# A scan kernel of two layers: the phases of layer 0 in another order, one more joint pair of row scans in layer 1, the last column quarter summed by halves

## The chip, the core and the metric

One core of a Trainium2 chip runs the whole program. The metric is the device time of one execution in microseconds (us), lower is better; it is given as the median of several runs. TensorE (PE in the profile, its weight loads PEld) does the matrix products, VectorE (DVE), ScalarE (ACT) and GpSimd (POOL) work element by element, and transfers are issued from the queues of SyncE (SP), ACT and POOL.

## The reference

Two layers of the same kind, on x of 32 images, 48 channels, 64 rows, 128 columns, in float32:

```
x = x + scans(groupnorm(x))          # 16 groups of 3 channels, per image; twice, with other weights
step:  next = inp + conv1d(carry, w, 5 taps, 48x48 channels, padding 2) + b
scans: D: down over the 64 rows;  U: up again over D's rows, same weights
       R: right over the 128 columns of U;  L: left over R
```

Each step needs the step before it, so a layer is a chain of 63 + 63 steps over rows and 127 + 127 over columns. Images are independent of each other, and U must be complete over the rows before R can begin for the same images.

## The kernel before, in words

**Work.** The images are four groups of eight. A row scan takes one group: a row of it is three tiles of 128 partitions (48 channels times 8 places along the convolved direction, 384 in all) by 128 elements. A column scan takes a pair of groups, and a column of it is of the same size. A step (`step`, L941 to L970) is nine products, each in two matmul instructions, and three additions on VectorE (L968), which add bias and input and write the next row or column in place. The next step's products read it.

**Phases.** `PHASES` lists twelve phases: four row phases (down and up for one group) and two column phases (right and left for a pair) in each layer. Layer 0 goes rows 0, rows 1, columns of pair 0, rows 2, rows 3, columns of pair 1. Layer 1 does all rows first. The step tiles are named after it: step_02d is layer 0, group 2, down; step_01r is layer 0, pair 1, right. A phase in `JOINED` shares its down scan with the up scan of the phase before: one joint step does both, with 256 elements in each product, by the same weights (`two_row_step`). Before, phases 8 and 9 are joined: group 2 down with group 1 up, and group 3 down with group 2 up, in layer 1.

**Memory.** The scanned data lie in three slots of SBUF. A row phase holds rows 0 to 31 of its group in one slot and rows 32 to 63 in another; the three slots change roles from phase to phase. A column phase takes the 128 columns in four quarters of 32; each quarter has six units (three tiles, times the two groups of the pair, its halves). What leaves the slots goes to DRAM and comes back in another layout: the normalized input (xin), the rows after U (upa in layer 0, upb in layer 1), the result of layer 0 (mid).

**The seam.** Where a column phase follows the second row phase of its own pair (`follows`), its first quarter cannot be read from DRAM in time. The first rows are then sent from slot to slot directly (`send_row`, `send_rest`: transfers arena<-arena) when the up scan ends. This is so for both column phases of layer 0 before, and for none in layer 1.

**The order of all other work.** `at(t, fn)` writes a task into an agenda; t counts steps, a joint step as two. Before each step the tasks that are due are issued, and every engine and queue keeps that order (`in_order`). An engine waits at a task for its data, with all that stands behind it. The tasks that matter here:
- `plan_input` (L1089): brings one group of x in. Six blocks of four rows per partition: `take_in` (one transfer arena<-in_x, into the one buffer), `permute` on GpSimd (L712), `put_out` (xin<-arena), and `take_others` on ScalarE (L583 sums, L575 squared deviations). Then `scaling`, a chain of small operations spread over about ten steps; it begins with a sum over ScalarE's results on VectorE (L600) and, where its slack is 0, goes on there with L605, which needs the squares as well.
- `plan_rows` (L1109): loads the rows of a group in four parts of 16 rows (`move_rows`: 20 transfers arena<-xin each), scales them on ScalarE (`scale_rows`, L797: 24 instructions for 16 rows), and writes the rows after U (`move_rows`: ten transfers upa<-arena per 8 rows). I call one such transfer a piece.
- `plan_cols` (L1169): loads and spills quarters; for each unit, the residual is loaded and added on GpSimd (L889), the result kept in mid, and its statistics taken for the next layer's normalization: half 0 on VectorE (L628), half 1 on ScalarE (`ResultStatsA`: L651, L654, L657, eight plus one plus eight instructions for a unit).

## Time and profile before

| | |
|---|---|
| runs | median 4161.74 us of 3, from 4159.11 to 4164.88 |
| profiled execution | 4154.44 us, of it 4152.7 between first and last instruction |
| mean granted clock of TensorE | 0.987 |
| VectorE, ScalarE, GpSimd busy | 2075.8 us (50%), 1307.4 (31%), 832.1 (20%) |
| transfers | 680.86 MB, of 2213904 packets 2014096 under 512 B |

The profiled execution is 7.3 us below the median of the runs. A step of a scan is seen in the profile as 18 matmuls on L954 and three VectorE operations on L968. The time of a scan without waits is its number of steps times the time of a step; anything above that is a wait, and the idle time noted in brackets in the timeline, with what ended it, says of whom. A row of a timeline has the start, the length, the engine, the line, the operation, what it writes and reads, the count, and in brackets the idle time before it. A row of the table by stretches has the borders, the length, then busy time and number of instructions for PE, PEld, DVE, ACT, POOL, the granted clock, the share of the DMA engines and GB/s.

### The profile page before, as it was taken

The numbers are of one execution on the slowest core, as the hardware profiler recorded it, in microseconds if no ns is written. First come the engines' busy times: TensorE is split into PE (matmuls) and PEld (weight loads), VectorE is DVE, ScalarE is ACT, GpSimd is POOL, SyncE is SP. The second block draws the span as 40 slices with busy tenths as digits, with TensorE's granted clock in tenths as the row PEclk, the third lists the DMA queues.
The fourth block names the chain that finished last, engine by engine and source line by source line (L and its number), as shares of the span: only waits on it lengthen the run. The fifth ranks groups of instructions, "written<-read, shape, count | busy, mean of one in ns | idle before, by whom it ended". The sixth has DMA issues, their size and how long they took to land. (4 is left out here: it accounts for less than half of the span.)

```text
span 4152.7 us, 85830 instructions
## 1 busy us (share of the span) xinstructions
PE 4021.1 (97%) x34360; PEld 3934.6 (95%) x34360; DVE 2075.8 (50%) x6124; ACT 1307.4 (31%) x2630; POOL 832.1 (20%) x745
## 2 busy tenths in 40 slices
PE   6999989899999999999999999999999999999994
PEld 5999989899999999999999998888999999999994
DVE  6454444457655444445656443333444444444444
ACT  4646001436884500003584534443000002200122
POOL 5631010333421001002412000000000015610354
PEclk9999999999999999999999999999999999999997
DMA  9897779769978966913997975666599029999799
GB/s 298 223 188 147 121 129 211 225 150 277 198 189 179 146 115 117 216 41 93 255 172 145 141 114 95 99 104 105 95 167 216 1 59 256 302 241 154 147 234 194
DMA packets 2213904, 680.86 MB, mean 164 GB/s; under 512 B 2014096, under 2 KB 2162816, under 8 KB 2188928
## 3 DMA queue, kind: packets, MB, share of 16 engines
q1 hardware_dynamic: 2069376, 582.40, 68.4%
q10 hardware_dynamic: 141568, 87.46, 8.7%
q0 software_dynamic: 2560, 5.51, 0.5%
q8 instruction: 271, 4.44, 0.5%
q14 instruction: 129, 1.06, 0.1%
HBM read 398.32 MB, written 295.14 MB: 167 GB/s over the span
## 5 line engine op out<-in xcount | busy, mean ns | idle before, releaser
L889 POOL TENSOR_TENSOR arena<-arena 128x2048 f32<-128x2048 f32 x80 | 362.8, 4549 | 1519.5 <-PE step_10l L954 474.3
L797 ACT ACTIVATE arena<-arena,offsetr,scaler 128x128 f32<-128x128 f32 (+1 forms) x576 | 345.0, 688 | 352.5 <-DMA arena<-mid 244.6
L797 ACT ACTIVATE arena<-arena,offset,scale 128x256 f32<-128x256 f32 (+2 forms) x360 | 249.3, 788 | 155.7 <-DMA arena<-xin 131.7
L712 POOL COPY arena<-arena 128x256 f32<-128x256 f32 x340 | 200.9, 652 | 470.7 <-DMA arena<-in_x 451.5
L954 PE MATMUL step_00r<-arena,early 128*128 128x128 f32 x2286 | 254.3, 275 | 25.2 <-DVE arena L968 14.3
L954 PEld LDWEIGHTS step_00r<-arena,early 128*128 128x128 f32 x2286 | 253.1, 186 | 26.1 <-DVE arena L968 15.0
L651 ACT ACTIVATE early<-arena 128x256 f32<-128x256 f32 x192 | 129.5, 675 | 453.2 <-POOL arena L889 446.9
L954 PE MATMUL step_01r<-arena,early 128*128 128x128 f32 x2286 | 251.4, 273 | 6.9 <-DMA arena<-arena 5.4
L954 PEld LDWEIGHTS step_01r<-arena,early 128*128 128x128 f32 x2286 | 250.7, 185 | 7.6 <-issue 5.7
L954 PE MATMUL step_11r<-arena,early 128*128 128x128 f32 x2286 | 249.2, 272 | 0.0
L954 PEld LDWEIGHTS step_11r<-arena,early 128*128 128x128 f32 x2286 | 248.7, 184 | 0.5 <-DVE arena L968 0.3
L954 PE MATMUL step_10r<-arena,early 128*128 128x128 f32 x2286 | 248.7, 272 | 0.1
L954 PEld LDWEIGHTS step_10r<-arena,early 128*128 128x128 f32 x2286 | 248.5, 184 | 0.2 <-DVE arena L968 0.2
L954 PE MATMUL step_10l<-arena,wleft 128*128 128x128 f32 x2286 | 248.5, 272 | 0.0
L954 PE MATMUL step_11l<-arena,wleft 128*128 128x128 f32 x2286 | 248.5, 272 | 0.0
L954 PE MATMUL step_00l<-arena,wleft 128*128 128x128 f32 x2286 | 248.4, 272 | 0.0
L954 PE MATMUL step_01l<-arena,wleft 128*128 128x128 f32 x2286 | 248.4, 272 | 0.0
L954 PEld LDWEIGHTS step_10l<-arena,wleft 128*128 128x128 f32 x2286 | 248.4, 184 | 0.0
L954 PEld LDWEIGHTS step_11l<-arena,wleft 128*128 128x128 f32 x2286 | 248.4, 184 | 0.0
L954 PEld LDWEIGHTS step_00l<-arena,wleft 128*128 128x128 f32 x2286 | 248.4, 184 | 0.0
L954 PEld LDWEIGHTS step_01l<-arena,wleft 128*128 128x128 f32 x2286 | 248.4, 184 | 0.0
L911 ACT COPY arena<-arena 128x256 f32<-128x256 f32 x172 | 99.7, 656 | 360.5 <-POOL arena L889 249.5
(565 smaller groups left out, 6912.9 us busy)
## 6 DMA issues: line engine op xcount, KB each, us to landing
xin<-arena SPq DMA_DIRECT2D x94, 512.0 KB, 5.5
arena<-in_x SPq DMA_DIRECT2D x18, 2048.0 KB, 9.6
arena<-xin SPq DMA_DIRECT2D x96, 384.0 KB, 10.8
upb<-arena SPq DMA_DIRECT2D x192, 192.0 KB, 3.9
arena<-upb SPq DMA_DIRECT2D x96, 384.0 KB, 11.0
arena<-xin SPq DMA_DIRECT2D x174, 192.0 KB, 4.3
mid<-arena SPq DMA_DIRECT2D x32, 1024.0 KB, 11.7
upa<-arena SPq DMA_DIRECT2D x168, 192.0 KB, 3.9
```

What stands on the lines that cost most here:

```text
L651: nc.scalar.activation(junk[:, 0:n], view[:, b], AF.Identity, accum_out=self.sum[:, i, j : j + 1])
L712: copy(dst[:, r, q], src[:, r0 + r, q])
L797: nc.scalar.activation(args[0], args[0], AF.Identity, bias=args[2], scale=args[1])
L889: eng.tensor_tensor(unit, unit, nat, ALU.add)
L911: copy(by_w(perm)[:, a], src[:, a])
L954: nc.tensor.matmul(part(turn(whole(ps[o]))[0:m], -s), weights[:, i, at : at + m], part(turn(src(i)), s), start=seen[o] == 1, stop=seen[o] ...
```

## The change

Four things change. In layer 0 all four row phases come first, then both column phases, as in layer 1; so neither column phase follows the rows of its own pair, and the seam is used nowhere. In layer 1 phase 7 is joined too: group 1 down runs with group 0 up. The last quarter of the second column phase is added and measured by halves: the three units of half 1 right after the scan, those of half 0 later, since the joined phase 7 puts its first rows into the places of half 1. And the tasks get other times: groups 2 and 3 of the input are brought in during the row phases 01 and 02, six blocks 11.5 steps apart (13 before), each load 5.5 steps ahead of its permutation (7 before); the slack of the scaling of group 2 goes from 4 to 0; the weights of the columns and of layer 1 are loaded in later phases; where a row phase of layer 0 follows another, the first two parts of its rows are loaded three and four steps earlier and scaled two and three steps earlier.

```diff
 PHASES = (
     ("rows", 0, 0),
     ("rows", 0, 1),
-    ("cols", 0, 0),
     ("rows", 0, 2),
     ("rows", 0, 3),
+    ("cols", 0, 0),
     ("cols", 0, 1),
...
-JOINED = (8, 9)
+JOINED = (7, 8, 9)
...
             if g > 1:
-                at(t - 7, take_in, g, rows * j, nat)
+                at(t - 5.5, take_in, g, rows * j, nat)
...
-        spread(t, scaling(f"x{g}", 0, g, stats, (0, 0, 4, 0)[g]), 1)
+        spread(t, scaling(f"x{g}", 0, g, stats, 0), 1)
...
             if not PHASES[k][1]:
-                ahead, scaled = (-33, -22, 0, 11), (-16, -5, 16, 30)
+                ahead, scaled = (-36, -26, 0, 11), (-18, -8, 16, 30)
...
-            first, every = left + 34 + 32 * n_done, 4.5
-            if j == 0 and PHASES[k + 1 if not final else k][0] == "rows":
-                first, every = (end + 29, 6) if pair else (first, 7)
-            units += [(first + every * i, j, i) for i in range(n)]
+            first = left + 34 + 32 * n_done
+            times = [(first + 4.5 * i, i) for i in range(n)]
+            if j == 0 and not final and PHASES[k + 1][0] == "rows":
+                times = [(end + 3 + 7 * i, 2 * i + 1) for i in range(NG)]
+                times += [(end + 28 + 6 * i, 2 * i) for i in range(NG)]
+            units += [(t, j, i) for t, i in times]
...
-            spread(units[-1][0] + (14 if pair else 70), pair_scaling(pair, stats, 8), 1)
+            spread(units[-1][0] + 14, pair_scaling(pair, stats, 8), 1)
...
-    times = [starts[1] + 36] + [starts[2] + 45 + 13 * j for j in range(5)]
+    times = [starts[1] + 24 + 11.5 * j for j in range(6)]
     plan_input(2, times, 6, 6, nats, tiles[2:4])
-    times = [starts[2] + 116 + 13 * j for j in range(2)]
-    times += [starts[3] + 42 + 13 * j for j in range(4)]
+    times = [starts[2] + 24 + 11.5 * j for j in range(6)]
     plan_input(3, times, 6, 6, nats, tiles[2:4])
...
-    at(starts[1] + 50, more_weights, "right", 0, RIGHT)
-    at(starts[1] + 54, more_weights, "left", 0, LEFT)
-    at(starts[3] + 50, more_weights, "down1", 1, DOWN)
+    at(starts[3] + 50, more_weights, "right", 0, RIGHT)
+    at(starts[3] + 54, more_weights, "left", 0, LEFT)
+    at(starts[5] + 70, more_weights, "down1", 1, DOWN)
```

Two places show what this does to the order. The first is ScalarE where layer 1 begins (10d). L797 is the scaling of group 0's rows; L651, L654 and L657 together are the statistics of one unit of half 1 (sum_r, neg_r, dev_r). Before:

```order
L797 ACTIVATE arena<-arena,offsetr_12864,scaler_12863 128x256 x24
L651 ACTIVATE early,sum_r_117<-arena 128x256 x8
L654 ACTIVATE neg_r_118<-sum_r_117 128x8
L657 ACTIVATE early,dev_r_119<-arena,neg_r_118 128x256 x8
L797 ACTIVATE arena<-arena,offsetr_12864,scaler_12863 128x256 x72
```

With the change, at the same place, the third unit and what follows it (the scaling of rows 0 to 15 with a unit of the quarter before, the scaling of rows 16 to 31, and the first two units of half 1 stand ahead of these rows):

```order
L651 ACTIVATE early,sum_r_117<-arena 128x256 x8
L654 ACTIVATE neg_r_118<-sum_r_117 128x8
L657 ACTIVATE early,dev_r_119<-arena,neg_r_118 128x256 x8
L797 ACTIVATE arena<-arena,offsetr_15678,scaler_15677 128x256 x48
L797 ACTIVATE arena<-arena,offsetr_15678,scaler_15677 128x128 x72
```

Before, the 72 scalings of rows 16 to 63 stand in one run, with the three units of half 1 behind them; now 24 of them (rows 16 to 31) stand ahead of the three units, and 48 (rows 32 to 63) behind.

The second is SP's queue where the input blocks of a group are fetched (in_x is x, xin2 and xin3 the normalized layout of groups 2 and 3, upa1 the rows of group 1 after U). Before, the blocks of group 2, during the right scan of pair 0:

```order
L288 DMA arena_72<-in_x 128x8x512
L288 DMA xin2_82<-arena_72 128x4x256 x4
L288 DMA arena_72<-in_x 128x8x512
L288 DMA xin2_82<-arena_72 128x4x256 x6
L288 DMA arena_72<-in_x 128x8x512
L288 DMA xin3_83<-arena_72 128x4x256 x2
```

With the change, ahead of the second block of group 3, during 02d:

```order
L288 DMA xin3_83<-arena_72 128x4x256 x2
L288 DMA upa1_89<-arena_72 48x32x32 x2
L288 DMA upa1_89<-arena_72 32x32x32
L288 DMA upa1_89<-arena_72 16x32x32
L288 DMA upa1_89<-arena_72 48x32x32 x2
L288 DMA upa1_89<-arena_72 16x32x32
L288 DMA upa1_89<-arena_72 48x32x32 x2
L288 DMA upa1_89<-arena_72 32x32x32
L288 DMA arena_72<-in_x 128x8x512
```

The input blocks now share the queue with the pieces of the row phases: between the last write of xin2 and the second block of group 3 stand 80 pieces arena<-xin2, 70 pieces upa1<-arena, the first block and two writes of xin3.

## The prediction

> **What bounds the kernel now.** I read the page first, then a table by stretches cut where the first matmul of each scan starts, then the timeline of each engine around every step that is longer than its neighbours. TensorE is busy 97% of the span, so only its steps and the waits between them count.
>
> ```profile
> span 4152.7 us, 85830 instructions
> ...
> 323.87:448.30 124.43, 124.43 (x1136) 124.43 (x1135) 60.58 (x189) 56.06 (x92) 11.78 (x19) 1.00 0.67 125
> 448.30:583.67 135.37, 124.59 (x1137) 124.43 (x1135) 60.94 (x190) 0.00 (x0) 15.67 (x31) 0.98 0.85 143
> 583.67:852.62 268.95, 254.54 (x2294) 253.82 (x2295) 123.31 (x388) 75.58 (x200) 58.45 (x103) 0.97 0.77 197
> 852.62:1100.91 248.29, 248.29 (x2289) 248.29 (x2288) 159.91 (x452) 142.10 (x336) 92.32 (x40) 1.00 0.87 213
> 1100.91:1358.32 257.41, 253.44 (x2291) 252.60 (x2289) 142.27 (x458) 168.58 (x347) 68.80 (x78) 0.99 0.83 185
> 1358.32:1614.17 255.85, 250.50 (x2282) 250.03 (x2281) 122.13 (x382) 53.94 (x73) 17.19 (x37) 1.00 0.77 127
> 1614.17:1867.01 252.84, 251.26 (x2286) 250.73 (x2287) 121.87 (x380) 0.19 (x1) 0.00 (x0) 0.99 0.56 128
> 1867.01:2115.29 248.28, 248.28 (x2288) 248.28 (x2287) 159.62 (x451) 129.63 (x303) 81.50 (x18) 1.00 0.69 176
> 2115.29:2240.76 125.47, 125.37 (x1136) 124.80 (x1135) 73.16 (x212) 95.81 (x179) 29.23 (x8) 1.00 0.86 162
> 2240.76:2367.99 127.23, 127.23 (x1160) 126.62 (x1159) 66.46 (x227) 46.95 (x69) 4.26 (x13) 1.00 0.82 136
> 2367.99:2493.18 125.19, 125.19 (x1137) 124.80 (x1136) 60.85 (x189) 55.38 (x88) 0.00 (x0) 1.00 0.73 115
> 2493.18:2734.57 241.39, 241.39 (x1136) 206.95 (x1135) 88.62 (x191) 100.07 (x192) 0.50 (x1) 1.00 0.62 98
> ...
> 3100.53:3349.16 248.63, 248.57 (x2288) 248.38 (x2287) 122.34 (x381) 0.00 (x0) 0.00 (x0) 1.00 0.45 102
> ```
>
> In order these are 01d, 01u, 00R, 00L, 02d with 02u, 03d with 03u, 01R, 01L, 10d, 10u, 11d, the joint 11u/12d, and 10R. 01d shows a row scan without waits: 124.43 for 63 steps, 1.975 a step. 10R (248.63) and 00L (248.29) show a column scan without. The rest is above that, and the timeline of PE names the waits: the seam (a transfer arena<-arena ends it), twice, and a wait for VectorE late in 00R.
>
> ```profile
> 583.67 16.05 PE L954 MATMUL step_00r<-arena,early 128*128 128x128 f32 x126 [10.78 <-DMA arena<-arena]
> ...
> 821.95 14.30 PE L954 MATMUL step_00r<-arena,early 128*128 128x128 f32 x108 [12.63 <-DVE arena L968]
> ...
> 836.23 11.97 PE L954 MATMUL step_00r<-arena,early 128*128 128x128 f32 x108
> ...
> 1614.17 14.27 PE L954 MATMUL step_01r<-arena,early 128*128 128x128 f32 x108 [5.35 <-DMA arena<-arena]
> ```
>
> VectorE was itself held there by the statistics of input group 2: its first small operation (L600) stood in its queue until ScalarE's sums were there. After the wait six steps (108 matmuls) took 14.30 us against 11.97 a little later, so a wait of this size costs 2.3 more.
>
> ```profile
> 820.61 0.20 DVE L600 TENSOR_REDUCE mean_x_x<-sum_x_x 128x8 f32<-128x48 f32 x1 [12.86 <-ACT early L583]
> ```
>
> **The change part by part.** *What goes.* From 323.87 to 2115.29 are 1791.4 us. With no new wait the same scans take six row scans at 124.43, two R at 248.63 and two L at 248.29: 1740.4. The small products of the scalings remain: 10u with one result scaling is 127.23 against 124.43, so 2.8; an input scaling, by 00u, 1.4, twice.
>
> ```profile
> 198.00:323.87 125.87, 125.62 (x1145) 125.42 (x1143) 63.87 (x211) 70.44 (x150) 40.27 (x69) 1.00 0.92 199
> ```
>
> That makes 1746.0, a gain of 45.4. The new joint pair replaces 10u and 11d (252.4) by a joint scan (241.39) with the result scaling of 2.8 in it: a gain of 8.2. Sum: 53.6.
>
> *Wait A, the statistics of input group 3.* It was fetched in 00R and 02d/02u, group 2 mostly in 00R; now each has one row phase, and the queue also carries that phase's pieces. What a piece costs the queue, and what a block costs, shows around 02u and 03d:
>
> ```profile
> 1275.55 0.37 SPq L288 DMA_DIRECT2D arena<-in_x  x1
> 1275.97 18.13 SPq L288 DMA_DIRECT2D xin<-arena  x6
> ...
> 1305.60 21.10 SPq L288 DMA_DIRECT2D arena<-xin  x20
> 1326.80 21.17 SPq L288 DMA_DIRECT2D upa<-arena  x20
> ...
> 1380.00 44.70 SPq L288 DMA_DIRECT2D arena<-xin  x40
> ```
>
> ```profile
> 814.63 9.32 POOL L712 COPY arena<-arena 128x256 f32<-128x256 f32 x16 [12.06 <-DMA arena<-in_x]
> ...
> 835.50 4.78 POOL L712 COPY arena<-arena 128x256 f32<-128x256 f32 x8 [6.53 <-DMA arena<-in_x]
> ...
> 1284.28 9.44 POOL L712 COPY arena<-arena 128x256 f32<-128x256 f32 x16 [12.29 <-DMA arena<-in_x]
> ```
>
> ```profile
> 1297.28 0.21 DVE L605 TENSOR_TENSOR neg_x_x<-neg_x_x,mean_x_x 128x48 f32<-128x48 f32 x1 [1.28 <-ACT early L575]
> ```
>
> A piece takes 1.06 us (21.10/20). A block lands 8.7 after its issue (1284.28 less 1275.55), its statistics are done 13.0 later (1297.28), and since there is one buffer, the next is issued then: 21.5 a block, as the 20.9 between 814.63 and 835.50 show. The last put of a group is issued by 1294.1, about 13 after its block landed with its own transfer.
>
> Group 2 first. The queue comes free at 370.6 (the row below), block 0 lands at 379 and is measured by 392; rows 48 to 63 are scaled (17.95) until 410, block 1 until 423; four more at 21.5 give 509, and some 6 for blocks that queue behind pieces give 515. VectorE comes to L605 at step 35 of 01u: 448.3 + 35 x 1.975 + 0.5 = 518. No wait, by 3.
>
> ```profile
> 328.35 42.26 SPq L288 DMA_DIRECT2D arena<-xin  x40
> ...
> 344.66 17.95 ACT L797 ACTIVATE arena<-arena,offset,scale 128x256 f32<-128x256 f32 x24 [13.15 <-DMA arena<-xin]
> ```
>
> Group 3: the last block of group 2 landed at 502, its put at 515; then 80 + 70 pieces at 1.06 are 159, two puts 3, so block 1 of group 3 is issued at 677, lands at 686, the last lands four periods later at 772 and is measured by 785. 02d starts at 448.3 + 124.4 + 1.4 = 574.1, and L605 comes 97 steps later: 766.2. VectorE waits 19 and every step behind it; with 2.3 for the restart, A costs **21**. Its bounds: a transfer that moves next to nothing takes the queue 0.42 (a row of the mask, below); 150 of those are 63, and A is gone. At 1.12 a piece (44.70/40) it is 30.
>
> ```profile
> 371.41 0.42 SPq L288 DMA_DIRECT2D spread_r<-in_mask  x1
> ```
>
> I take 1.06, since all pieces shown lie within 1.05 to 1.12. The Trainium skill (DMA: Bandwidth & Descriptors, Issuing engines are not separate DMA queues) says that the time on the sequencer to start a transfer is usually small relative to the transfer; by that the queue would be through its pieces early, A would be 0 and the sum 21 lower. The trace disagrees for these pieces, at 1.06 one behind the other. Rows 32 to 47 of group 2 just arrive: 80 pieces after 515 is 600, their scaling began 18.8 after that point in 03d (1398.79, below, less 1380.00) and takes 18, so 637 against the need at 574.1 + 31 x 1.975 + 1 = 636: no cost. After A, the rows of 03d have the 19 us that TensorE lost, and none is late.
>
> ```profile
> 1398.79 17.95 ACT L797 ACTIVATE arena<-arena,offset,scale 128x256 f32<-128x256 f32 x24 [15.61 <-DMA arena<-xin]
> ```
>
> *Wait B, the halves.* In 10d the three units of half 1 now stand ahead of the scaling of rows 32 to 63 on ScalarE.
>
> ```profile
> 2063.78 0.68 ACT L651 ACTIVATE early<-arena 128x256 f32<-128x256 f32 x1 [21.15 <-POOL arena L889]
> ...
> 2077.67 0.67 ACT L651 ACTIVATE early<-arena 128x256 f32<-128x256 f32 x1
> ...
> 2122.73 29.83 ACT L797 ACTIVATE arena<-arena,offsetr,scaler 128x256 f32<-128x256 f32 x40
> 2161.38 6.07 ACT L797 ACTIVATE arena<-arena,offsetr,scaler 128x256 f32<-128x256 f32 x8 [8.82 <-PE step_10d L954]
> ```
>
> One unit takes 13.9 (2077.67 less 2063.78). ScalarE has been busy since 2063.8, with work that the change leaves as it is; it begins rows 16 to 31 at 2122.7 and ends them at 2140.7 (17.95); three units end at 2182.3, rows 32 to 47 at 2200. Step 31 needs row 32 at 2115.3 + 31 x 1.975 + 1 = 2177.5. The wait is 22; with the restart B costs **24**. Bounds: 11 with the restart if only the first of the three tiles (6.07) held the step, 42 if the whole run of 48 had to end first. The code scales rows 32 to 47 in all three tiles first, and the step needs all three, so 24. Rows 48 to 63 follow at 2218, and step 47, moved by the wait, comes at 2234: no second wait.
>
> *The rest* I cost at nothing. The column weights of layer 0 are loaded at the end of 03d and due at the end of 03u; their cover is 03u's 125 us, and without it 00R would start up to 64 later (two times 30 transfers at 1.06). The data of the first quarters are in DRAM a phase before they are read; 10R, with the same order, stands at 248.63 without a wait. The added waits on POOL and SP hold up only the pieces behind them, which are in the sums of A.
>
> Sum: 53.6 - 21 - 24 = 8.6 less. The profiled execution (4154.4) is 7.3 below the median of the runs; against the median the change gives 4161.7 - 8.6 = **4153.1**.
>
> **The rivals.** *A is hidden.* The queue works ahead of its tasks and is through the 150 pieces before the blocks are due, and 29.6 less remain: 4132. For it: 0.42 for a transfer next to nothing. Against: no twenty pieces above took less than 1.05 each. The page named above would have it so. *B is hidden.* 32.6 less, 4129: if the additions of half 1 came so late that ScalarE had nothing else to do. But then it waits in its order, so B would only grow. *Both are hidden*: 53.6 less, 4108. Two chains worked out from different engines would both have to be wrong. *Slower: blocks land late.* One block before took 15.7, issued at 1190.89 in a full queue and used at 1206.60:
>
> ```profile
> 1190.89 1.27 SPq L288 DMA_DIRECT2D arena<-in_x  x1
> ...
> 1206.60 9.50 POOL L712 COPY arena<-arena 128x256 f32<-128x256 f32 x16 [34.40 <-DMA arena<-in_x]
> ```
>
> If the five blocks behind the first take 12.2 instead of 8.7, half way to that, A grows by 17 and the time is 4161.7 + 9 = 4171. At 15.7 it is 4188. It decides from 3.4 us more a block. Against it: no residual or mid transfers stand in the queue in these phases now.
>
> **How the numbers follow.** My forecast has 0.50, A hidden 0.16, B hidden 0.09, both 0.07, late blocks 0.18. 0.2%, about what a measurement of this kernel can tell from no change, is 8.3 us, which is where the forecast stands: half of it counts as faster, half as same. Of the late blocks I put 0.08 to same. Faster: 0.25 + 0.16 + 0.09 + 0.07 = 0.57; same: 0.25 + 0.08 = 0.33; slower: 0.10. The range reaches from one hidden wait with the other 5 smaller (4124) to the slow rival at 12.2 (4171); it leaves out both hidden and the worst of the late blocks.
>
> **What would show it.** Right: no idle before the first step of 00R and 01R; a joint scan of about 244 in place of 10u and 11d; PE idle about 19 in 02u, ended by VectorE behind L605 and ScalarE's squares; PE idle about 22 at row 32 of 10d, ended by ScalarE's L797. Wrong: either idle time missing or half as large, or a new one in 01u (group 2 late), at rows 32 of 02d or 03d, or in the second joint scan, where the pieces of three groups meet.

## The result, and the profile after

The changed kernel takes 4178.76 us (median of 5 runs, 4172.91 to 4181.02), the kernel before 4159.11 on the same chip: a ratio of 1.0050, with an interval of 1.0039 to 1.0061. The change makes it 0.5% slower; 4153.1 was forecast. Its profiled execution takes 4175.82 us, of it 4174.1 of span, against 4154.44 and 4152.7 before: 21.4 more, where the sum said 8.6 less. Two executions of the kernels below ran at a clearly lower granted clock (4614.57 us at 0.846 and 4405.27 us at 0.887); all medians and ratios leave them out.

The table by stretches of the changed kernel, cut at the first matmul of each scan: 01u, 02d, 02u, 03d, 03u, 00R, 01R, 10d, then the three joint scans 10u/11d, 11u/12d and 12u/13d. The columns are those of before; the last three are granted clock, share of the DMA engines and GB/s.

```profile
452.82:584.53 131.71, 128.90 (x1144) 128.52 (x1143) 67.03 (x211) 55.70 (x124) 28.90 (x49) 0.97 0.95 199
584.53:708.96 124.43, 124.43 (x1137) 124.43 (x1135) 60.59 (x189) 71.57 (x120) 15.02 (x26) 1.00 1.00 180
708.96:864.74 155.78, 130.75 (x1145) 130.07 (x1144) 64.25 (x211) 77.38 (x179) 44.12 (x74) 0.90 0.78 185
864.74:989.43 124.69, 124.69 (x1136) 124.54 (x1135) 60.38 (x189) 51.90 (x70) 0.00 (x0) 1.00 0.89 137
989.43:1113.86 124.43, 124.43 (x1137) 124.43 (x1136) 60.43 (x189) 0.00 (x0) 0.50 (x1) 1.00 0.88 152
1113.86:1362.17 248.31, 248.31 (x2288) 248.31 (x2287) 122.38 (x381) 0.00 (x0) 0.00 (x0) 1.00 0.58 122
...
1610.45:1861.89 251.44, 251.44 (x2312) 250.73 (x2311) 140.54 (x442) 39.87 (x100) 31.91 (x19) 1.00 0.68 167
...
2110.18:2258.73 148.55, 128.60 (x1136) 127.73 (x1135) 77.33 (x242) 117.05 (x222) 30.77 (x12) 0.92 0.86 160
2258.73:2508.26 249.53, 246.12 (x1161) 209.53 (x1160) 89.88 (x199) 93.63 (x180) 2.75 (x9) 0.99 0.56 89
2508.26:2752.77 244.51, 241.95 (x1136) 206.77 (x1135) 88.62 (x192) 100.12 (x193) 0.50 (x1) 1.00 0.65 104
2752.77:2999.50 246.73, 243.99 (x1135) 207.84 (x1134) 88.57 (x192) 90.79 (x174) 0.51 (x1) 0.99 0.65 102
```

Both seams are gone: 00R takes 248.31 (268.95 before), and 01R has only the 3.1 of its statistics. New waits are in 01u, 02u, 10d and the joint scans, which take 740.8 together where 727.0 (244.2 + 2 x 241.4) was forecast. VectorE's timeline says who ends them:

```profile
527.68 0.21 DVE L605 TENSOR_TENSOR neg_x_x<-neg_x_x,mean_x_x 128x48 f32<-128x48 f32 x1 [2.55 <-ACT early L575]
...
797.43 0.20 DVE L600 TENSOR_REDUCE mean_x_x<-sum_x_x 128x8 f32<-128x48 f32 x1 [22.74 <-ACT early L583]
...
804.45 0.21 DVE L605 TENSOR_TENSOR neg_x_x<-neg_x_x,mean_x_x 128x48 f32<-128x48 f32 x1 [5.22 <-ACT early L575]
...
2182.61 0.35 DVE L968 SCALAR_TENSOR_TENSOR arena<-step_10d,bd,arena 128x128 f32<-128x128 f32 x1 [10.04 <-ACT arena L797]
2194.39 0.61 DVE L968 SCALAR_TENSOR_TENSOR arena<-step_10d,bd,arena 128x128 f32<-128x128 f32 x2 [11.42 <-DMA arena<-xin]
...
2325.51 0.45 DVE L454 RECIPROCAL dev_r<-dev_r 128x48 f32<-128x48 f32 x1 [5.73 <-ACT dev_r L442]
```

The first is group 2's statistics, late in 01u. The next two are wait A, 28 us instead of 19. The fourth and fifth are wait B, in its place and of its size: 10d is 148.55 against 125.47. The fifth names a DMA, but ScalarE scales there from 2176.6 to 2200.4 us without a gap, eight instructions of 6 us to a tile, and the wait ends as its third tile is done. The last, in the first joint scan, was not in the sum; I call what the joint scans lose **wait C**.

Against the forecast the profiled execution is 30 longer. Of that, 4.5 lies ahead of 328.39 us, mostly in 00d, whose code is the same and which took from 135.0 to 140.7 us in the kernels of this study, so it is not the change's; 14.8 is layer 0 (group 2's 5.8 and 8.9 more of A), 12.8 is layer 1 (13.8 of C, 0.9 less of B); the rest of the program is 2 shorter.

### The profile page after: what moved, and what is told of

It reads as the page before. It is cut to its first block, busy times and chain, and to the rows that moved or that the text cites. A ratio compares the mean times of both kernels' runs of the same rounds, so it can differ in the third digit from the quotient of the medians.

```text
span 4174.1 us, 83112 instructions
## 1 busy us (share of the span) xinstructions
PE 4022.4 (96%) x33226; PEld 3898.0 (93%) x33226; DVE 2046.4 (49%) x5951; ACT 1334.9 (32%) x2724; POOL 788.7 (19%) x672
## 3 DMA queue, kind: packets, MB, share of 16 engines
q14 instruction: 125, 1.02, 0.1%
## 5 line engine op out<-in xcount | busy, mean ns | idle before, releaser
L797 ACT ACTIVATE arena<-arena,offsetr,scaler 128x128 f32<-128x128 f32 (+1 forms) x672 | 373.0, 644 | 458.7 <-DMA arena<-mid 341.2
L651 ACT ACTIVATE early<-arena 128x256 f32<-128x256 f32 x192 | 129.7, 675 | 803.1 <-POOL arena L889 796.8
L797 ACT ACTIVATE arena<-arena,offset,scale 128x256 f32<-128x256 f32 (+2 forms) x360 | 249.3, 787 | 192.2 <-DMA arena<-xin 181.9
```

What stands on the lines that cost most here:

```text
L651: nc.scalar.activation(junk[:, 0:n], view[:, b], AF.Identity, accum_out=self.sum[:, i, j : j + 1])
L797: nc.scalar.activation(args[0], args[0], AF.Identity, bias=args[2], scale=args[1])
```

## The experiments

**The theories.** Mine, after the result: SP's queue issues in order, and blocks, rows and weights stand in it behind other pieces; a better order, or another queue, takes the waits away. Rival one: the 16 DMA engines behind all queues are full in these scans, and then no order helps, the wait only moves. Rival two: ScalarE's own order (scalings ahead of statistics) makes the waits.

Every kernel is the changed one with the edit shown. Ratios are to the kernel before on the same chip, with their interval; the changed kernel's is 1.0050.

### Wait C: weights_late, seven_alone, upb_pool

```diff
-    at(starts[6] + 50, more_weights, "right", 1, RIGHT)
-    at(starts[6] + 54, more_weights, "left", 1, LEFT)
+    at(starts[9] + 128, more_weights, "right", 1, RIGHT)
+    at(starts[10] + 40, more_weights, "left", 1, LEFT)
```

> Only the loads of layer 1's column weights differ from the changed kernel: those for right go from the end of 10d to the start of 13u, those for left into 10R. This takes some 60 short transfers, about 30 us of SP's queue, out of the first joint scan. My theory, that the queue is behind in the joint scans: the waits at steps 15 and 16 of the first joint scan and those at the starts of the two later ones go, 740.8 us for the three become about 730, and the time falls by about 11 to 4168. Rival, that the joint scans wait for something else (ScalarE's order, or the transfers themselves): the three stay within 3 us and so does the time.

In the changed kernel SP's queue looks like this at the start of the first joint scan:

```profile
2239.66 25.81 SPq L288 DMA_DIRECT2D arena<-mid  x40
2265.52 3.36 SPq L288 DMA_DIRECT2D taps<-in_w  x5
2269.05 13.79 SPq L288 DMA_DIRECT2D early<-taps  x25
2282.88 3.04 SPq L288 DMA_DIRECT2D taps<-in_w  x5
2286.08 12.68 SPq L288 DMA_DIRECT2D wleft<-taps  x25
2298.87 26.87 SPq L288 DMA_DIRECT2D arena<-mid  x52
```

From 2265.5 to 2298.8 no row piece is issued; ScalarE waits for rows, its square root for the statistics (L442) stands behind that scaling, and VectorE behind the square root. With the weights moved, the three joint scans read:

```profile
2263.58:2508.02 244.44, 244.44 (x1160) 208.51 (x1159) 89.97 (x199) 105.36 (x202) 2.75 (x9) 1.00 0.63 100
2508.02:2749.41 241.39, 241.39 (x1135) 207.02 (x1134) 88.87 (x192) 99.93 (x192) 0.50 (x1) 1.00 0.65 103
2749.41:2990.81 241.40, 241.40 (x1135) 207.02 (x1134) 88.88 (x192) 79.50 (x152) 0.51 (x1) 1.00 0.59 94
```

No wait is left, in the two later scans either; 727.2 in all. The time is 4166.11, ratio 1.0019 (1.0009 to 1.0028). Wait C is 33 us of weights in a queue without room for them.

```diff
-JOINED = (7, 8, 9)
+JOINED = (8, 9)
```

> The changed kernel with only phases 8 and 9 joined, as before; the halves of the last quarter keep their new order. My theory: the wait in 10d stays (about 148 us); 10u, 11d and the two joint scans take 735, as in the kernel before, against 740.8 for the three joint scans now, so the third joint pair has earned nothing and the time is about 4173, 6 us less. Rival, that the joint pair is worth the 8.2 us of my sum and the added waits have another cause: the time is about 4187.

Measured: 4171.37, ratio 1.0037 (1.0023 to 1.0052). 10u and 11d take 127.23 and 125.24, the two joint scans 241.42 and 241.39: 735.3, against 740.8 with three joint scans and 727.2 with these and the weights moved. The joint pair is worth 8.1 us, as in the sum, and C took more than that from it.

```diff
-                        dma(there, here)
+                        dma(there, here, nc.gpsimd if layer else None)
```

> Only the queue of the pieces upb<-arena (the rows after U of layer 1, 320 in all) differs from the changed kernel: they are issued from GpSimd's queue instead of SP's. Some 60 to 93 pieces of 0.92 us leave SP's queue in each joint scan. Theory, that SP's queue is what is full there: the three joint scans, 740.8 us in all, go to about 727 (as 244.4 + 241.4 + 241.4, which they have with the weights moved), and the time falls by 13 to about 4166. Rival, that the 16 DMA engines behind the queues are full and a piece costs its time there, from whichever queue: the pieces arena<-mid then take more than their 0.48 us each on SP, the three scans stay within 4 us, and so does the time. A second rival, that GpSimd's queue is so slow to issue that the rows come late for 10R: a wait at the start of 10R that was not there.

```profile
2267.00:2522.39 255.39, 246.65 (x1160) 209.88 (x1159) 89.97 (x199) 112.93 (x217) 61.62 (x79) 0.98 0.59 103
2522.39:2763.79 241.40, 241.40 (x1136) 207.02 (x1135) 88.90 (x192) 105.48 (x202) 67.51 (x81) 1.00 0.61 108
2763.79:3005.18 241.39, 241.39 (x1135) 207.02 (x1134) 88.90 (x192) 66.17 (x127) 67.51 (x81) 1.00 0.49 90
```

The second and third joint scan lose their waits with the weights still in place: there the queue was the limit, and the engines, at a share of 0.65 before, take the same pieces from two queues (at 0.61 and 0.49). The first scan, where the weights stand, got 6 longer (255.39) and takes most of the 8 us back: 4177.85, ratio 1.0050 (1.0036 to 1.0064). My theory holds for two scans of three; why the first got longer is not shown.

### Wait A: seven kernels

Scans of the same code differ from one execution to the next. Nine of the kernels have the layer 0 of the changed one (the changed one itself, layer0_only, and those of waits B and C without early_joint). In their profiles 01u took 131.7 to 137.2, 02u 150.1 to 160.2, both together 286.6 to 294.0, and the six scans 01d to 03u 784.5 to 792.0. A difference inside these bounds tells nothing.

```diff
-        dma(nat, src[:, :, r0 * W : (r0 + n) * W])
+        dma(nat, src[:, :, r0 * W : (r0 + n) * W], nc.scalar if g > 1 else None)
```

> The loads of the input blocks of groups 2 and 3 (18 loads arena<-in_x in all, 12 of them these) are issued from ScalarE's queue instead of SP's; nothing else differs from the changed kernel. My theory, that the blocks came late because they stood behind row pieces in SP's queue: the wait in 02u (scan 155.8 us) and the one in 01u (131.7) go down to the 125.9 that 00u has, together 36 us, and the time goes from 4179 to about 4143. Rival, that the transfers themselves were slow because the DMA engines are full with pieces: the blocks land no earlier, 01u and 02u stay within 8 us of what they were, and the time stays above 4165. Rival, that ScalarE's own work is what was late: the same, with ScalarE busy without a gap ahead of the wait.

Measured: 4172.58, ratio 1.0044 (1.0030 to 1.0058). 01u falls to 125.90 as my theory has it, but 02u grows from 155.78 to 168.38. The two scans are 294.3 against 287.5: no better. The first block of group 3 was issued at 629.75 us, after ScalarE, which issues now, had waited 25.7 us for rows; that is 24 earlier than in the changed kernel, but it is measured at 666.25, as there (666.83), behind the scaling of rows 32 to 63. The puts still stood in SP's queue, behind 20 pieces that took 42.34 us. This is not the engines' pace: for 22.6 of these SP's queue stood still, by the trace until block 1 (issued at 679.35) had landed, and in the first 13.4 of them the engines' share was 0.19. So this run brought a wait of its own and does not tell a full queue from full engines.

```diff
-                t = t_up + 29 + 5 * (H - h1) / E8 + (34 if h1 <= HALF else 0)
+                t = t_up + 29 + 5 * (H - h1) / E8 + ((50 if k == 1 else 34) if h1 <= HALF else 0)
```

> Only the pieces upa<-arena of the lower half of group 1 move: 16 steps later, so that the first 20 of them stand behind block 1 of group 3 in SP's queue and not ahead of it; all else is the changed kernel. Theory, that the order in SP's queue sets when a block is fetched: block 1 is issued about 20 us earlier (it was at 694), the wait in 02u falls from 31.4 above a scan without waits to about 12, and the time by about 19 to 4160. Rival, that the DMA engines are full and the pieces cost the later blocks what block 1 gains: the last block lands within 6 us of where it did (791 with the same start), and the time changes by less than 6.

Measured: 4184.38, ratio 1.0066 (1.0051 to 1.0081), no faster, with 02u at 162.14. Block 1 of group 3 was issued at 677.6 instead of 694.1, as planned. But the pieces, now behind it, held blocks 2 and 3 (issued 33 and 30 us after the one before), and the last block went out at 787.3, in the changed kernel at 783.2. The order changed, the sum did not, as rival one has it; but a queue that is full would do the same.

```diff
-        t += work + lag + (0, 2, 2, 1)[g]
+        t += work + lag + (0, 2, 10, 10)[g]
...
-                ahead, scaled = (-36, -26, 0, 11), (-18, -8, 16, 30)
+                ahead, scaled = (-36, -26, 0, 11), (-9, 0, 16, 30)
```

> The scaling chains of groups 2 and 3, which begin with VectorE's wait for ScalarE's sums, are issued 8 and 9 steps later (about 16 and 18 us), and rows 0 to 31 are scaled later to suit; the loads, the blocks and the queues stay as they are in the changed kernel. Theory, that only VectorE's early place in its queue makes TensorE wait for these sums, and rows 0 have time: 01u goes from 131.7 to about 126, 02u from 155.8 to about 140, the time falls by about 22 to 4157. Rival, that rows 0 to 31 are then late by what is gained: 02d and 03d (124.4 and 124.7) grow by as much at their first rows or at row 16, and the time stays.

Here 02d, 02u and 03d read:

```profile
575.30:710.01 134.71, 126.26 (x1136) 126.07 (x1135) 60.66 (x189) 71.90 (x121) 15.36 (x27) 0.97 0.99 175
710.01:847.39 137.38, 129.72 (x1144) 129.07 (x1143) 64.27 (x211) 75.05 (x175) 43.88 (x74) 0.96 0.75 191
847.39:989.97 142.58, 128.49 (x1137) 127.95 (x1135) 60.66 (x189) 53.69 (x72) 0.00 (x0) 0.95 0.91 137
```

02u gained 18 us, 16 were forecast; 02d gave back 10 and 03d 18, waiting for rows 16 and 32. In the changed kernel these rows were in time only because TensorE was late. 4175.77, ratio 1.0045 (1.0031 to 1.0058). So the wait is not VectorE's early place; the pieces come no sooner.

```diff
-        dma(nat, src[:, :, r0 * W : (r0 + n) * W])
+        dma(nat, src[:, :, r0 * W : (r0 + n) * W], nc.gpsimd if g > 1 else None)
...
-                dma(x_put(source[0][g], r + i), one.rearrange("p (q n) -> p q n", q=NQ))
+                there = x_put(source[0][g], r + i)
+                dma(there, one.rearrange("p (q n) -> p q n", q=NQ), nc.gpsimd if g > 1 else None)
```

> For groups 2 and 3 of the input, the loads arena<-in_x and the puts xin<-arena are issued from GpSimd's queue, next to the permutation that stands between them; SP's queue keeps the row pieces alone. All else is the changed kernel. Theory, that the blocks are late because they stand behind pieces in SP's queue: 01u goes from 131.7 to 125.9 us and 02u from 155.8 to about 128, with no new wait, and the time goes from 4179 to about 4145. Rival, that the 16 DMA engines themselves are full there (their share is 0.95 in 01u and 1.00 in 02d of the changed kernel): the pieces on SP take longer than 1.06 us each, rows come late, and waits appear at row 32 of 02d or 03d; the six scans 01d to 03u, 785.5 us in all, stay within 12 of that, and the time above 4165.

02d and 02u, and ScalarE ahead of the first block's statistics (L583):

```profile
575.22:708.62 133.40, 126.36 (x1136) 126.17 (x1135) 60.62 (x189) 78.66 (x138) 15.72 (x24) 0.97 0.98 167
708.62:858.84 150.22, 128.59 (x1144) 128.20 (x1143) 67.23 (x211) 68.21 (x157) 54.75 (x86) 0.92 0.71 175
```

```profile
627.54 17.86 ACT L798 ACTIVATE arena<-arena,offset,scale 128x256 f32<-128x256 f32 x24 [24.48 <-DMA arena<-xin]
648.54 17.94 ACT L798 ACTIVATE arena<-arena,offset,scale 128x256 f32<-128x256 f32 x24 [3.14 <-DMA arena<-xin]
666.38 0.62 ACT L583 ACTIVATE early<-arena 128x512 f32<-128x512 f32 x1
```

01u lost its wait, 02d has one of 9 at row 32, 02u keeps 24; the six scans 01d to 03u make 784.2, before 785.5, inside the rival's 12. 4173.99, ratio 1.0046 (1.0034 to 1.0059). A queue of its own did not help the blocks. And the rows show what the chain of A really is: the first block of group 3 was issued at 513.26 and had landed by 526.97, but it is measured only at 666, behind the scaling of rows 32 to 63, which waits for pieces. In the changed kernel it is the same, at 666.83. So the chain runs from the pieces (120 between 527 and 654 us in the changed kernel), through ScalarE's order, into six blocks.

The share of the DMA engines says why the pieces are slow. In 02d of the changed kernel:

```profile
DMA packets 129860, 22.36 MB, mean 180 GB/s; under 512 B 125751, under 2 KB 127799, under 8 KB 129847
...
q1 hardware_dynamic: 129847, 22.18, 99.3%
```

All 16 engines are full at 180 GB/s, with 172 bytes a packet. They were nearly full where I had read the price of a piece, too: from 328.35 to 370.61 us in the kernel before, where almost nothing but 40 pieces moves, their share is 0.96, at 150 GB/s and 128 bytes a packet. A piece has 192, 128 or 64 KB, 154 on average; at 150 GB/s that is 1.05 us. This is the price of 1.06 that I had put down to the queue. The pieces of layer 0 themselves were never put on two queues, so that such a split gains nothing there is not shown.

```diff
+            if k == 1 and h0 >= HALF:
+                continue
             at(t, move_rows, k, h0, h1, True)
...
```

> The changed kernel without the 40 pieces upa<-arena of rows 32 to 63 of group 1 (those rows after U are not kept; one plain copy in 03d fills their place with other data, so the output differs). They stand among the 140 pieces ahead of group 3's first blocks. Theory, that the wait in 02u is the sum of the pieces' transfer times: rows 48 to 63 of group 2 are there some 40 us earlier, the first block with them, and 02u falls from 155.8 to below 131. Rival, that the six blocks of 21.5 us each are too long a chain in themselves: 02u stays above 145. The time itself is not compared, as 03d has the copy.

```profile
707.55:833.43 125.88, 125.62 (x1145) 125.43 (x1143) 63.86 (x211) 52.77 (x116) 28.74 (x47) 1.00 0.84 228
```

This is 02u. With 40 pieces less ahead of it, A is gone altogether (125.88, as 00u has it), though the six blocks are the same, and the last four are still issued 21.6 to 23.2 us apart: ScalarE measures the first at 624 instead of 667 us. It is the sum of the transfers ahead, not the length of the chain alone; whether the queue or the engines set their pace, this run does not tell.

What could help, then, is to do work in an engine's idle time, not to reorder full ones. On top of input_pool and of layer0_only (below), blocks_early brings group 3's blocks 15 steps forward, ahead of the 24 us in which ScalarE sat idle:

```diff
-    times = [starts[2] + 24 + 11.5 * j for j in range(6)]
+    times = [starts[2] + 9 + 11.5 * j for j in range(6)]
...
-        t += work + lag + (0, 2, 2, 1)[g]
+        t += work + lag + (0, 2, 2, 16)[g]
```

> Differs from layer0_input_pool in the times of group 3's input blocks alone: all six 15 steps earlier, so that ScalarE measures the first one ahead of rows 32 to 47 of 02d and the second ahead of rows 48 to 63; the scaling chain stays where it was. In input_pool the first block was measured only at 666 to 680 us, behind the scaling of rows 32 to 63, for whose pieces ScalarE sat idle 24 us. Theory, that ScalarE's order holds the blocks: the last block is done some 30 us earlier, 02u goes from 146.0 to about 127. The two blocks (9 us each) then go ahead of rows 32 to 63 on full DMA engines, so 02d grows from 130.8 by up to 15. In all 5 to 15 us less than layer0_input_pool's 4143. Rival, that the engines are all there is: what 02u gains 02d and 03d lose, and the time stays within 4 of 4143.

02d, 02u and 03d:

```profile
574.32:714.47 140.15, 126.68 (x1136) 126.30 (x1135) 60.67 (x189) 98.40 (x192) 36.80 (x59) 0.95 0.97 198
714.47:840.35 125.88, 125.62 (x1145) 125.43 (x1144) 63.88 (x211) 56.60 (x116) 33.69 (x52) 1.00 0.86 177
840.35:965.03 124.68, 124.68 (x1136) 124.53 (x1135) 60.46 (x189) 45.33 (x61) 0.00 (x0) 1.00 0.85 128
```

4125.72, ratio 0.9932 (0.9918 to 0.9945), against 0.9972 of layer0_input_pool: some 17 us less, a little more than expected. ScalarE measures the first block at 600 us now, and the six scans make 765.5. So ScalarE's order was part of A (rival two); whether the earlier times alone, without the other queue, would do the same was not tried. both_early then does the same for group 2 and brings its first rows forward, into 01u, where SP's queue was empty for 50 us:

```diff
-    times = [starts[1] + 24 + 11.5 * j for j in range(6)]
+    times = [starts[1] + 9 + 11.5 * j for j in range(6)]
...
-        t += work + lag + (0, 2, 2, 16)[g]
+        t += work + lag + (0, 2, 17, 16)[g]
...
+                if k == 2:
+                    ahead = (-49, -39, 0, 11)
```

> Differs from blocks_early in group 2: its input blocks are 15 steps earlier too, and the first 32 rows of group 2 are loaded 13 steps earlier, in the second half of 01u, where SP's queue of blocks_early stands idle from 464 to 517 us. Theory, that what is left of the wait, 15.7 us in 02d at row 32, comes from the sum of pieces between 517 and 633 us: with 40 of them earlier, rows 32 to 47 arrive some 15 to 30 us earlier, 02d falls from 140.2 to about 126, and the time from 4126 to about 4112. Rival, that the blocks and pieces of 01d and 01u then collide on full engines: 01d or 01u grows by as much (124.4 and 125.9 in blocks_early), and the time stays within 4 of 4126.

```profile
574.10:706.86 132.76, 126.63 (x1137) 126.44 (x1135) 60.58 (x189) 75.27 (x155) 35.47 (x57) 0.97 0.98 199
```

4112.57, ratio 0.9897 (0.9884 to 0.9911). The time is as forecast, by half the mechanism and so partly by luck: 02d fell by 7, not by 14 (row 32 still waits 8), and the other 6 us between the medians, which are from two chips, are not accounted for by these scans. This is the best version of the study, 1.0% faster than the kernel before.

### Layer 0 alone: layer0_only, layer0_input_pool

```diff
-JOINED = (7, 8, 9)
+JOINED = (8, 9)
...
-                times = [(end + 3 + 7 * i, 2 * i + 1) for i in range(NG)]
-                times += [(end + 28 + 6 * i, 2 * i) for i in range(NG)]
+                times = [(end + 29 + 6 * i, i) for i in range(n)]
```

> The change to layer 0 alone: order of the phases, times of the input, rows and weights as in the changed kernel; in layer 1 phases 8 and 9 alone are joined and the last quarter of the second columns has the order and the times of the kernel before. Theory: the seams' 45 us are won, of which the waits in 01u and 02u take about 36; 10d is back at 125.5. The time is about 4148, some 9 less than the kernel before. Rival, that 10d's wait has its cause in layer 0 (the column phases now stand close together): 10d stays above 140 and the time at about 4171, as with only phases 8 and 9 joined.

Measured: 4147.76, ratio 0.9987 (0.9979 to 0.9996), with 10d at 125.49, 01u at 136.87 and 02u at 154.39. The new order of layer 0 is worth what is left of the seams' 45 us after A and group 2, and wait B is not its doing.

> layer0_only and input_pool together. If SP's queue is what delays the input blocks: about 4148 less 34, 4114, which would be 43 less than the kernel before. If the DMA engines are full: about what layer0_only gives, within 10.

Both edits: 4143.43, ratio 0.9972 (0.9964 to 0.9981), within 10 of layer0_only. Here 01u takes 129.57, 02d 130.84, 02u 146.05, 03d 130.68: again the wait spread over four scans rather than gone.

### Wait B: five kernels

> Only ScalarE's order at the start of layer 1 differs from the changed kernel: rows 32 to 47 are scaled behind the first unit of half 1, rows 48 to 55 behind the second, rows 56 to 63 behind the third. My theory: the wait at row 32 of 10d goes and 10d falls from 148.6 us to about 125. SP's queue is then no less occupied than before, so that part of the 24 us can come back in the three joint scans (740.8 us in all); if the queue is the bound there they get up to 24 longer and the time stays near 4175, if it only lags at a few places they stay within 5 and the time is about 4155. Rival, that row 32 waits for its pieces rather than for ScalarE: 10d stays above 140.

```diff
+                    at(t0 + 8, scale_rows, k, 32, 48)
...
+                    at(t0 + 15, scale_rows, k, 48, 56)
+                    at(t0 + 35, scale_rows, k, 56, 64)
```

Measured: 4189.64, ratio 1.0082 (1.0068 to 1.0096). This kernel scales rows 48 to 55 ahead of their load, so the load waits for the scaling (SP's queue for 23.4 us); it tells nothing of B. The next one has the order that was meant:

```diff
-                at(t0 + scaled[i], scale_rows, k, i * LOAD, (i + 1) * LOAD)
+                if k == 6 and i == 2:
+                    at(t0 + 8.5, scale_rows, k, 32, 48)
+                elif k == 6 and i == 3:
+                    at(t0 + 24.5, scale_rows, k, 48, 56)
+                    at(t0 + 35, scale_rows, k, 56, 64)
+                else:
+                    at(t0 + scaled[i], scale_rows, k, i * LOAD, (i + 1) * LOAD)
...
-                    at(t + 1, stats[1].take, j, o, unit)
+                    at(t + (8 if t == end + 17 else 1), stats[1].take, j, o, unit)
```

> What rows_first was meant to be: ScalarE scales rows 32 to 47 behind the first unit of half 1, rows 48 to 55 behind the second, with the third unit held until those rows have been loaded; nothing is scaled ahead of its load now. Theory: ScalarE would reach rows 32 to 47 at 2149, end them at 2167, before step 31 needs row 32 (2172.5), so that 10d falls from 148.6 to about 126 us. SP's queue has the same pieces in less time, so that part comes back in the three joint scans (740.8): up to 22 us longer if the queue is full through all of them, by which the time would stay near 4178; if only the weights were one load too many, up to 10, and the time is about 4165. Rival, that row 32 waits for its pieces: 10d stays above 140.

10d, and ScalarE at the last tile of rows 32 to 47:

```profile
2109.78:2260.49 150.71, 133.60 (x1137) 132.53 (x1135) 77.96 (x242) 123.87 (x248) 30.75 (x12) 0.93 0.85 158
```

```profile
2172.75 5.99 ACT L797 ACTIVATE arena<-arena,offsetr,scaler 128x256 f32<-128x256 f32 x8 [10.90 <-DMA arena<-mid]
```

ScalarE is ahead now, and waits 10.9 us for the pieces of that tile. The wait of 22 at row 32 became three, of 7, 5 and 10 at rows 32, 48 and 56 (the next expectation names the whole steps, 2 more each), and 10d is no shorter: 4179.55, ratio 1.0061 (1.0044 to 1.0078). My theory of ScalarE's order alone falls; the rival, that row 32 waits for its pieces, holds for 7 of the 22.

residuals_pool adds to rows_between the late weights and moves the residuals and results of the second columns to GpSimd's queue:

```diff
-                dma(here, x_by_col(t, e, j)[c0:c1])
+                dma(here, x_by_col(t, e, j)[c0:c1], nc.gpsimd if pair else None)
...
-            dma(there, by_line(quarter(k, j)[:, half, o])[p0:p1])
+            dma(there, by_line(quarter(k, j)[:, half, o])[p0:p1], nc.gpsimd if pair else None)
```

> Three edits to the changed kernel together: the order on ScalarE of rows_between, the late weights of weights_late, and the residuals (arena<-xin) and kept results (mid<-arena) of the second column phase of layer 0 issued from GpSimd's queue. Theory: in rows_between rows 32, 48 and 56 still waited 9, 7 and 12 us because their pieces come late in SP's queue, behind some 19 residuals and 8 results of about 17 us; without these 10d goes from 150.7 to about 130, the three joint scans are at 727, and the time is about 4147. Rival, that GpSimd, now late with its additions, holds up the units of half 1 and so the first rows of phase 7, or that the DMA engines are full in 10d (share 0.86): 10d stays above 143 or the first joint scan begins with a wait, and the time stays above 4160.

The end of 01L and the start of 10d in it, by stretches:

```profile
2063.93:2111.99 48.06, 48.06 (x445) 48.06 (x443) 35.49 (x96) 43.89 (x90) 31.11 (x25) 1.00 1.02 257
2111.99:2165.00 53.01, 32.46 (x292) 31.94 (x290) 16.15 (x49) 29.05 (x55) 38.73 (x24) 0.83 1.01 230
```

The waits at rows 32, 48 and 56 are gone, but row 16 waits 25: 10d is 152.86, the time 4170.62, ratio 1.0045 (1.0031 to 1.0058). From two queues the engines are full for 100 us, and the row pieces among them now come later. The rival with the full engines was right here, as in layer 0.

halves_old is weights_late with the `times` of layer0_only and the third joint pair kept.

> weights_late with the last quarter of the second columns in the old order (six units in turn, both halves mixed, from 29 steps after the scan on); the third joint pair stays. Theory, that the halves are the price of the joint pair, since its first rows go into the places of half 1: 10d is back at 125.5, but the last unit of half 1 is measured only about 67 steps after 01L, the first rows of group 1 come behind it, and the first joint scan begins with a wait of 20 to 30 us; the time stays within 6 of 4166. Rival, that the halves were not needed: no such wait, and about 4142.

Measured: 4204.84, ratio 1.0119 (1.0104 to 1.0134), with 10d at 153.30 and the first joint scan at 282.03. In this kernel the first rows of group 1 are loaded ahead of the additions of half 1, into the same places, so it mixes data and its order is not the one I meant to test. That the halves are needed for the joint pair stays argued from the code: in the old order the last unit of half 1 would be measured some 60 of 10d's 63 steps in.

early_joint: both_early's layer 0, with layer 1 of weights_late.

> Layer 0 as in both_early, layer 1 as in the changed kernel (phase 7 joined, the last quarter by halves) with the late weights of weights_late. Theory: layer 1 does here what it did behind the other layer 0: 10d at about 149 instead of 125.5, the joint pair 244.4 instead of 252.4, the other joint scans 241.4 each; so about 15 us more than both_early. Rival, that the wait in 10d came from the delays of layer 0: 10d at about 126 and 8 us less than both_early.

10d, and the first joint scan:

```profile
2077.73:2228.22 150.49, 128.36 (x1137) 127.52 (x1136) 77.33 (x242) 117.10 (x222) 28.86 (x10) 0.92 0.87 161
2228.22:2472.48 244.26, 244.26 (x1160) 208.50 (x1159) 89.91 (x199) 105.45 (x203) 2.77 (x9) 1.00 0.63 100
```

4129.32, ratio 0.9937 (0.9924 to 0.9950): 16.7 more than both_early, 15 expected. Wait B belongs to the halves that come with the third joint pair, whatever layer 0 does (seven_alone, with the halves and without the pair, has it too, 10d at 148.05), and costs three times the 8 us that the pair is worth.

## Why the prediction was wrong

- *What goes*, 45.4 + 8.2: right. No seam is left, and the joint pair takes 244.44 where 244.2 was forecast, once C is away.
- *Wait A*: right in place and in the engine that ends it, 29.9 instead of 21. The step that failed is "A piece takes 1.06", kept for every piece because "all pieces shown lie within 1.05 to 1.12". They had been read where no block was moving. Beside blocks and puts, as the rows of SP's queue below show, 20 pieces took 25.75 and ten 17.92, at shares of 1.03 and 0.96. So the blocks of group 2 went out 22 to 33 apart, not 21.5, and instead of a margin of 3 it had a wait of 6; block 1 of group 3 was issued at 694, not 677 (of these 17 us, 4.5 came from ahead of 328.39 and 8 from group 2's late blocks; the 150 pieces and two puts between took 167 instead of 162). I priced a queue; what was full were the engines. By the table the six scans 01d to 03u hold 682 us of the engines' time (share times length, with 0.73 for 01d), in the 747 that they would last without waits. That is not yet too much: both_early has the same sum, 681, in scans of 758.5. But in the changed kernel it is unevenly spread, 0.73 in 01d and 1.00 in 02d, and the chain of group 3 starts in 02d.

```profile
654.03 0.64 SPq L288 DMA_DIRECT2D arena<-in_x  x1
654.77 25.75 SPq L288 DMA_DIRECT2D upa<-arena  x20
...
694.10 0.62 SPq L288 DMA_DIRECT2D arena<-in_x  x1
...
696.11 17.92 SPq L288 DMA_DIRECT2D upa<-arena  x10
```

- *The rule of the Trainium skill*: I weighed one clause of DMA: Bandwidth & Descriptors, Issuing engines are not separate DMA queues (the time to start a transfer is usually small beside the transfer itself), and set the section aside because pieces took 1.06. They do not speak against it: at a share of 0.96 the 1.06 were the engines' pace. The section's first statement, that transfers from all issuing engines run and interleave on the same 16 DMA engines, was the one that mattered. residuals_pool agrees with it: from two queues the shares were 1.02 and 1.01, and row 16 waited 25 us. input_pool fits it (six scans of 784.2 after 785.5) but does not decide, since its first block of group 3 lay on the chip from 527 us on and waited for ScalarE.
- *Wait B*, 24: 23.1, and row 32 waited as worked out. That ScalarE alone made it was half the cause; the pieces of the same rows were 7 late themselves, so that taking ScalarE out of the way gained nothing.
- *The rest at nothing*: this failed for layer 1, with 13.8 us of C. I looked only at the weights that the change moves, and not at those it leaves where they are, for whose 33 us the third joint pair takes away the room. By SP's timeline the second joint scan issues 399 transfers in 224 of its 244.5 us: a piece arena<-mid at 0.47, a piece upb at 0.93, and some 0.05 between two. The queue has no room there even without weights; that a wait in the second joint scan would be a sign of error I had written down.
- *The rivals*: none of the hidden waits. The slower one had the right sign and, at 4171 to 4188, the size, but not the mechanism: blocks landed 8 to 11 us after their issue, near the 8.7 assumed; they were issued late.

## What to carry to other kernels

Before moving work from one stage to another, add up what every queue and the DMA engines have to do in the stage it goes to, not only what stands ahead of the one transfer in question. Here the stage at a share of 1.00 (02d) was the one whose chains came late. Where the engines were full, another order within the stage or another queue moved a wait and did not remove it, so judge an edit by the sum over the neighbouring scans, and against what the same code gives from one execution to the next. What helped was starting earlier, where the table shows a lower share, an idle engine or an idle queue, or issuing from a second queue where the share is low (the joint scans).

## What the runs showed of the hardware

- The time that SP's queue spends on a transfer was of two kinds. In the second joint scan of the changed kernel a piece arena<-mid took 0.46 to 0.47 us on average, whether it had 16, 32 or 48 KB, at a share of the engines of 0.52 to 0.64 in these stretches; there the queue was the limit, and another queue for upb took two scans' waits away. Where the share was 0.96 to 1.03 the time followed the engines: 1.06 us for a piece of 154 KB on average at 150 GB/s, and 1.79 each for ten issued just behind a block.
- Full engines moved 150 GB/s with row pieces almost alone (kernel before), 180 in 02d and 257 and 230 in the two stretches of residuals_pool, by what they carried; GB/s alone does not show that they are full, their share does.
- GpSimd issued ten pieces upb<-arena in 8.60 us, about as long as SP takes (0.93 each).
